# VectorE's block sums, folds and joins in a woven order, and product 5 of the last two batches in blocks

## The chip, the cores and the metric

The kernel runs on one core of one Trainium2 chip. The metric is the device time of one launch in microseconds (us), the median of repeated runs. The four engines that compute are TensorE (PE in the profile), VectorE (DVE), ScalarE (ACT) and GpSimd (POOL). Data moves in DMAs that are issued from the queues of SyncE (SP), of ScalarE and of GpSimd. Each engine works through its own list of instructions in the order in which the program emits them.

## The reference, cut to what matters

It is one cross attention over 8 batches. All arrays are float32: `x1` and `x2` are (8, 512, 1024), the inner width is D = 64.

```python
q = einsum('bcn,dc->bnd', x1, Wq) + bq
k = einsum('bcn,dc->bdn', x2, Wk) + bk[:, None]
v = einsum('bcn,dc->bdn', x2, Wv) + bv[:, None]
attn = softmax(einsum('bnd,bdm->bnm', q, k), axis=2)
return einsum('bcm,bnm->bcn', v, attn) + x1
```

## The kernel before, in words

**Two products per batch.** The kernel doesn't build v. For each batch it multiplies `x2` with the exponentials of the scores (stage "y", contraction 1024) and then `Wv` with the result (stage "o", contraction 512); the division by the softmax's sums falls in between, and the bias and `x1` are added at the end. Both stages cut their matrices into 2 x 2 quarters and use Winograd's form of Strassen's product: seven products of quarters in place of eight, named 1, 2, 6, 7, 5, 3, 4 in `MULT` (L355). The left operands are the quarters `11`, `12`, `21`, `22` of `x2` and their sums `S1` to `S4`; the right operands are the quarters of the exponentials `e` and their sums `T1` to `T4`. VectorE makes most of these sums.

**Blocks.** A stage-y product can be done plainly (`multiply`, L365: 16 matmul records of 128x512) or in blocks, which is the same seven-product form once more inside it: 28 records of 128x256. Blocks need eight more sums: four 128x256 ones on the left (`inner_left`, L412, each reading one or two made just before it) and three on the right (`inner_right`, L421: a 128x1024 one for `T1` and `T3` together, then `T2` from `T1`, then `T4` from `T2`). Their partial results go through two PSUM tiles, "chain" and "third", that share two buffers with the score tiles. `multiply_seeded` (L459) serves products 1, 2, 7, 3 and starts a pair of banks; `multiply_onto` (L489) serves 4 and 5 and adds to banks that are in use. Both return `complete`, one more VectorE sum. Before the change, product 5 runs in blocks in batches 1 to 5 only (`five` in `period`, L764), and plainly in batches 0, 6 and 7.

**The softmax.** Scores are taken for two halves `h` of the queries in four tiles each; ScalarE copies them to SBUF. VectorE folds the four tiles into a maximum with three steps of 128x1024 (`fold`, L242) and one of 128x512 (`fold_halves`, L250); GpSimd then takes the maximum over partitions (`highest`, L254). `lower` (L290) subtracts it, ScalarE exponentiates. Sums go the same way: for half 0, GpSimd's accumulating DMAs add the tiles (`add_tile`, L619) and VectorE folds once; for half 1 VectorE does the folds. `total` (L260) sums over partitions on GpSimd and sends the row to `few`, 4 numbers per partition. `invert` (L269) takes reciprocals of `few` on VectorE and sends them to DRAM; `spread` (L275) broadcasts them to all partitions; `shares` does both.

**The period.** `period` (L764) is emitted once per batch `s` and also holds the scores and exponentials of the next batch `n`, and the projections of queries and keys of the one after (`nn`). There are no due times and no planner: the order is written out by hand. TensorE's order in a middle batch is: products 1, 2, 6 of stage y; scores of half 0 of `n`; queries of `nn`; products 5, 7, 3; scores of half 1 of `n`; keys of `nn`; product 4; then the seven of stage o, in the order 1, 6, 2, 5, 7, 3, 4 (in the last batch 1, 6, 2, 5, 7, 4, 3). Batch 6 has no `nn`, so neither projection runs in it; batch 7 has no `n` either.

**Between the stages**, VectorE joins the seven results (`evict_y`, `evict_t3`, the two sums at the end of `multiply_4`), scales each quarter `y` by the reciprocals (`scale_y`, L544) and sums them (`sum_y`, L343). Product 2 of stage o reads the quarter `y["21"]`, which is joined last of all and scaled by `scale_y(s, "21")`.

Of the kernel before, what the change touches and what calls it, by code (L numbers as in the profile page):

```python
# [1 line left out]

# [9 lines left out]
ALU = mybir.AluOpType  # L12
# [3 lines left out]
def kernel(  # L16
# [47 lines left out]
    nc = tc.nc  # L64
# [81 lines left out]
    def sum_a(s, *ks):  # L146
        for k in ks:
            if k != "S3":
                s.a[k] = sb.tile([P, MH, C // 2], F32, tag=f"a{k}", name=f"a{k}_{s.b}")
        left_sums(s.a, *ks)  # L150
# [91 lines left out]
    def fold(s, h, i, kind, op):  # L242

        e = s.e[h]
        if i == 1:
            s.mx[h] = sb.tile([P, 2, H], F32, tag="fold", name=f"{kind}_{s.b}_{h}", bufs=2)
        f = s.mx[h]
        nc.vector.tensor_tensor(f, e[:, :, 0, :] if i == 1 else f, e[:, :, i, :], op)  # L248

    def fold_halves(s, h, op):  # L250
        f = s.mx[h]
        nc.vector.tensor_tensor(f[:, 0, :], f[:, 0, :], f[:, 1, :], op)  # L252

    def highest(s, h, halves=True):  # L254
        if halves:
            fold_halves(s, h, ALU.max)
        s.top[h] = sb.tile([P, H], F32, tag="top", name=f"top_{s.b}_{h}", bufs=2)
        nc.gpsimd.partition_all_reduce(s.top[h], s.mx[h][:, 0, :], P, ReduceOp.max)  # L258

    def total(s, h):  # L260
        fold_halves(s, h, ALU.add)
        s.den[h] = sb.tile([P, H], F32, tag="den", name=f"den_{s.b}_{h}", bufs=2)
        nc.gpsimd.partition_all_reduce(s.den[h], s.mx[h][:, 0, :], P, ReduceOp.add)  # L263
        s.few[h] = sb.tile([P, H // P], F32, tag="few", name=f"few_{s.b}_{h}", bufs=2)
        nc.gpsimd.dma_start(
            s.few[h], s.den[h][0:1, :].rearrange("o (p f) -> o p f", p=P)
        )
# [66 lines left out]
            s.tmp[1] = sb.tile([P, 2, H], F32, tag="yT1", name=f"uy1_{s.b}")  # L334
        nc.scalar.copy(s.tmp[1][:, j, :], s.bank["a", j])

    def sum_e(s, *ks, of=(0, 2)):
        for i in of:
            part = {n: v[:, i : i + 2, :] for n, v in s.t.items()}
            for k in ks:  # L340
                right_sums(part, k)

    def sum_y(s, k):  # L343
# [68 lines left out]
    def inner_left(s, i, x, tag):  # L412

        v = {f"{p + 1}{q + 1}": x[:, ts(q, MH // 2), ts(p, P)] for p in range(2) for q in range(2)}
        sums = sb.tile([P, 4, MH // 2, P], F32, tag=tag, name=f"aI{i}_{s.b}")
        for z, (k, x, y, op) in enumerate(LEFT):
            v[k] = sums[:, z]
            nc.vector.tensor_tensor(v[k], v[x], v[y], op)  # L418
        s.inner[i] = v

    def inner_right(s, i, x, *tags):  # L421

        v = {
            f"{q + 1}{r + 1}": x[:, ts(q, MH // 2), ts(r, H // 2)] for q in range(2) for r in range(2)
        }
        last = 4 // len(tags)
        shape = [P, last, MH // 2, H // 2]
        sums = [sb.tile(shape, F32, tag=t, name=f"eI{i}{t}_{s.b}") for t in tags]
        both, t2, t4 = sums[0][:, 0:2], sums[-1][:, last - 2], sums[-1][:, last - 1]
        part = x.rearrange("p (q k) (r n) -> p q k r n", q=2, r=2)  # L430
        nc.vector.tensor_tensor(
            both, part[:, :, :, 1, :], part[:, 0].rearrange("p k r n -> p r k n"), ALU.subtract
        )
        nc.vector.tensor_tensor(t2, both[:, 0], v["22"], ALU.subtract)
        nc.vector.tensor_tensor(t4, v["21"], t2, ALU.add)
        s.inner[i, "t"] = v | {"T1": both[:, 0], "T3": both[:, 1], "T2": t2, "T4": t4}

    def inner_product(s, i, z, ps, opens, *copies):

# [80 lines left out]
    def multiply_4(s, hooks={}):  # L520

        d, complete = multiply_onto(s, 4, "u5" if s.b < B - 1 else "a21", "r", hooks)
        complete()
        nc.vector.tensor_tensor(s.tmp[6], s.tmp[6], d, ALU.add)

    def multiply_5(s, hooks):

        d, complete = multiply_onto(s, 5, "u5", "r", hooks)
        complete()
        for j in range(2):  # L530
            nc.vector.tensor_tensor(d[:, j, :], s.bank["a", j], d[:, j, :], ALU.add)
        s.tmp[5] = d

    def copy_7(s, j):
        if j == 0:
# [8 lines left out]
    def scale_y(s, *ks):  # L544
        for k in ks:
            rden = s.rden[k in ("T3", "22")].unsqueeze(1).to_broadcast([P, 2, H])
            nc.vector.tensor_tensor(s.y[k], s.y[k], rden, ALU.mult)  # L547
# [77 lines left out]
        nc.scalar.copy(s.mx[h], s.e[h][:, :, 0, :])  # L625

    def sums(s, h):
        for i in range(1, MH):
            fold(s, h, i, "sum", ALU.add)
        total(s, h)  # L630

    def head_queries(s, x_sb, h, bank=None):
# [33 lines left out]
    def head(s):  # L666
# [55 lines left out]
        for i, bank in ((2, "a"), (3, "c")):  # L722
# [1 line left out]
            for g in range(2):  # L724
                nc.vector.tensor_tensor(f[:, 0, :], f[:, 0, :], copy.ps[g], ALU.max)
            copy()
        highest(s, 0, halves=False)
        sum_a(s, "S1", "S2")
        more_queries(*tiles[1:])
        load_x(states[1], x1)  # L730
# [11 lines left out]
    def head_second(s, n):  # L742


        scores(s, 1, 3)()
        for i in range(2, MH):
            fold(s, 1, i, "max", ALU.max)
        queries(n)()
        load_x(n, x2)
        highest(s, 1)  # L750
        sum_a(s, "S3", "S4")
        for i in range(MH):
            exponentials(s, 1, i)
# [10 lines left out]
    def period(s, n, nn, nnn):  # L764

        late = s.b >= 1
        five = late and nn is not None

        def first(i):
            multiply(s, "y", i, s.a, s.t, MH)  # L770
# [7 lines left out]
        def next_queries():  # L778
            evict = queries(nn, "c0")
            load_x(nn, x2)  # L780
            if five:
                return evict
            evict()

# [2 lines left out]
            if nnn:  # L787
                load_x(nnn, x1)

        def scores_0():  # L790
            then = scores_and(n, 0, 1, "c", next_queries if nn else nothing)
            for i in range(1, MH):
                fold(n, 0, i, "max", ALU.max)
            highest(n, 0)
            return then

# [11 lines left out]
        if s.b == 0:  # L808
            first(1)
            head_second(s, n)  # L810
            sum_e(s, "T1", "T2")
            total(s, 0)
            load_a(n, "11")
            first(2)
# [7 lines left out]
            load_a(n, "21", "22")  # L822
            first(6)
            scores_0()
            inner_left(s, 4, s.a["22"], "a12")
            inner_right(s, 4, s.t["T4"], "eT2")
            inner_left(s, 3, s.a["S4"], "aI3")
            shares(s, 1)
            first(5)
            inner_right(s, 3, s.t["22"], "eT1")  # L830
            for i in range(MH):
                lower(n, 0, i)
            first(7)
# [3 lines left out]
            complete_3()  # L837
            evict_t3(s)
            evict_y(s, "22")
            scale_y(s, "11", "T3", "22")  # L840
        else:
            complete_1 = multiply_seeded(s, 1, "y11")
            sum_e(s, "T1", "T2")
            complete_1()
            for i in range(1, MH):
                fold(s, 1, i, "sum", ALU.add)
            total(s, 1)
            invert(s, 0)
            complete_2 = multiply_seeded(
# [8 lines left out]
                sum_e(s, "T3")  # L858
            sum_t4(s)
            first(6)  # L860
            inner_left(s, 7, s.a["S3"], "yT4")
            if five:
                inner_left(s, 5, s.a["S1"], "i2")
                inner_right(s, 5, s.t["T1"], "y21", "u1")
            sum_a(s, "S4")
            if n:
                evict_q = scores_0()
            spread(s, 0)
            shares(s, 1)
            inner_right(s, 7, s.t["T3"], "yT1", "yT2")  # L870
            inner_left(s, 3, s.a["S4"], "aI3")
            if five:
                multiply_5(s, {6: evict_q})
            else:
                first(5)
            inner_right(s, 3, s.t["22"], "eT1")
            if n:
                lower(n, 0, 0)
            complete_7 = multiply_seeded(s, 7, "y12")
# [2 lines left out]
            if n:  # L882
                for i in range(1, MH):
                    lower(n, 0, i)
            else:
                inner_left(s, 4, s.a["22"], "a12")
                inner_right(s, 4, s.t["T4"], "eT2")

            hooks = {2: lambda: copy_7(s, 0), 5: lambda: copy_7(s, 1)}
            if n:  # L890
# [14 lines left out]
            if nn:  # L905
                next_keys()
        if late and n:
            inner_left(s, 4, s.a["22"], "a12")
            inner_right(s, 4, s.t["T4"], "eT2")
        if late:  # L910
            scale_y(s, "11", "T3", "22")
        sum_y(s, "T2")
        sum_y(s, "T1")
        if s.b == 0:
            value_sums("S1", "S2")
            for i in range(1, MH):
                fold(n, 1, i, "max", ALU.max)
            highest(n, 1)
        hooks = {}
        if s.b == 0:  # L920
# [1 line left out]
        elif n:  # L922
            hooks = {6: lambda: add_exponential(2), 5: lambda: exponential(n, 0, 3)}
            if nn is None:
                hooks[7] = first_sum
        multiply_4(s, hooks)
        if late and n:
            negate(n, "S3")
        if n:
# [1 line left out]
        if nn:  # L931
            load_a(nn, "21", "22")
        evict_y(s, "21")
        scale_y(s, "21")
        sum_y(s, "T4")
        if late and n:
            for i in range(1, MH):
                fold(n, 1, i, "max", ALU.max)
            highest(n, 1)
            add_11(n, "S3")  # L940
        second(1)
        if s.b == 0:
            copy_first(n, 0)
# [14 lines left out]
        evict_o(s, "11")  # L958
        if n:
            add_tile(n, 0, 3)  # L960
            inner_left(n, 1, n.a["11"], "i2")
        second(5)
        if n:
            for i in range(2 if s.b == 0 else 0, MH):
# [4 lines left out]
            add_11(n, "S2")  # L969
        evict_o(s, "22")  # L970
        if n:
            inner_right(n, 1, n.e[0][:, 0], "yT1", "yT2")
            inner_left(n, 2, n.a["12"], "aS4")
            inner_right(n, 2, n.e[0][:, 1], "eT4")
            second(3)
            evict_o(s, "12")
            second(4)
            total(n, 0)
            evict_o(s, "21")
        else:  # L980
            second(4)
            evict_o(s, "21")
            second(3)
            evict_o(s, "12")
# [37 lines left out]
```

## Time and profile before

| | us |
|---|---|
| median of 3 runs | 682.16 (682.11 to 682.16) |
| the profiled execution's own time | 682.56 |
| its span, first to last instruction | 680.8 |
| TensorE busy | 672.1 (99%) |
| VectorE busy | 615.2 (90%) |
| ScalarE busy | 336.9 (49%) |
| GpSimd busy | 218.5 (32%) |

The profiled execution is 0.40 us above the median, and 1.76 us of its time lie outside its span. TensorE's granted clock is 1.000 throughout. TensorE is busy in nine tenths or more of nearly every slice of the span, and so is VectorE in most; which of the two sets the time in a batch has to be read from the waits of that batch. In the timeline, a bracket behind an instruction holds the idle time of its engine before it and what ended that idle time. The numbering of batches is from 0.

### The profile page before, as it was taken

What the parts mean: (1) busy time and instruction counts of PE and PEld (TensorE: products, weight loads), DVE (VectorE), ACT (ScalarE), POOL (GpSimd) and SP (SyncE); (2) the same over time, 40 slices, a digit from 0 to 9 for tenths busy, and PEclk for the clock granted to TensorE, in tenths of its full rate; (3) what the DMA queues carried; (4) which work ended last, traced back from release to release, by engine and by line L of the source; (5) the groups of instructions that cost most, each with busy time, mean ns of one, the idle gap of its engine ahead of it and who ended that gap; (6) DMA issues with size and microseconds to landing.
All of it is one profiled execution on the core that took longest, in us unless ns stands there. A gap on an engine that the chain in (4) does not pass through costs nothing.

```text
span 680.8 us, 7209 instructions
## 1 busy us (share of the span) xinstructions
PE 672.1 (99%) x2420; PEld 397.9 (58%) x2420; DVE 615.2 (90%) x763; ACT 336.9 (49%) x564; POOL 218.5 (32%) x182
## 2 busy tenths in 40 slices
PE   8999999999999999999999999999999999999997
PEld 5333554757547565566656576464854747556763
DVE  1999998899999999999999998999989979999884
ACT  2734266365554564544644637446475356553320
POOL 0124215251153502643125421344213451154100
PEclk9999999999999999999999999999999999999999
DMA  9656658967798759969499693996947985489503
GB/s 300 271 191 241 155 212 139 240 138 246 180 249 221 154 202 253 214 185 245 123 297 199 174 264 116 280 212 160 277 89 174 222 194 110 92 146 268 144 13 110
DMA packets 50772, 131.09 MB, mean 193 GB/s; under 512 B 5552, under 2 KB 7856, under 8 KB 50736
## 3 DMA queue, kind: packets, MB, share of 16 engines
q0 software_dynamic: 22464, 54.60, 44.7%
q1 hardware_dynamic: 27984, 75.64, 30.8%
q10 hardware_dynamic: 288, 0.39, 0.2%
q8 instruction: 19, 0.31, 0.2%
q14 instruction: 17, 0.14, 0.1%
HBM read 87.30 MB, written 16.81 MB: 153 GB/s over the span
## 4 chain that ended last, share of the span: by engine, by line
PE 84%; DVE 6%; DMA 5%; issue 2%; ACT 1%; SPq 1%; POOL 1%; DVEq 0%; POOLq 0%; ACTq 0%
PE ps_ya L380 11%; PE ps_oa L380 11%; PE ps_yc L442 8%; PE ps_oc L380 7%; PE ps_ya L442 6%; PE ps_s L228 5%; PE ps_o L400 4%; PE ps_o L380 4%; PE ps_k L181 3%; PE ps_q L181 3%; PE ps_i4chain L442 3%; PE ps_i3chain L442 3%; PE ps_i7chain L442 2%; PE ps_i1chain L442 2%; PE ps_i2chain L442 2%
## 5 line engine op out<-in xcount | busy, mean ns | idle before, releaser
L263 POOL PARTITION_ALL_REDUCE den<-sum x16 | 52.6, 3285 | 97.4 <-DVE few L271 60.3
L258 POOL PARTITION_ALL_REDUCE top<-max x16 | 37.6, 2352 | 126.3 <-DVE max L252 75.7
L380 PE MATMUL ps_ya<-eT,aS 128*128 128x512 f32 x176 | 77.5, 594 | 0.0
L293 DVE TENSOR_TENSOR e<-e,top 128x1024 f32<-128x1024 f32 x60 | 69.9, 1218 | 0.0
L620 POOL DMA_DIRECT2D sum<-e x21 | 32.1, 1530 | 108.7 <-ACT sum L625 42.0
L297 ACT ACTIVATE e<-e 128x1024 f32<-128x1024 f32 x60 | 61.8, 1058 | 4.7 <-DVE e L293 4.0
L380 PE MATMUL ps_oa<-yT,w_S 128*128 128x512 f32 x128 | 57.5, 592 | 0.0
L380 PE MATMUL ps_oc<-yT,w 128*128 128x512 f32 x128 | 57.4, 592 | 0.0
L380 PEld LDWEIGHTS ps_ya<-eT,aS 128*128 128x128 f32 x176 | 33.2, 190 | 40.1 <-issue 37.9
L237 ACT COPY e<-ps_s 128x1024 f32<-128x1024 f32 x46 | 45.6, 1032 | 9.0 <-PE ps_s L228 8.8
L228 PE MATMUL ps_s<-q,k 64*128 64x512 f32 x188 | 47.9, 608 | 0.9 <-ACT q L647 0.8
L380 PEld LDWEIGHTS ps_oa<-yT,w_S 128*128 128x128 f32 x128 | 24.3, 190 | 30.6 <-issue 30.6
L380 PEld LDWEIGHTS ps_oc<-yT,w 128*128 128x128 f32 x128 | 24.3, 190 | 30.6 <-issue 29.2
L248 DVE TENSOR_TENSOR max<-max,e 128x1024 f32<-128x1024 f32 x30 | 36.7, 1225 | 2.2
L391 ACT COPY uo<-ps_oa 128x512 f32<-128x512 f32 x32 | 18.7, 586 | 34.9 <-PE ps_oa L380 34.9
L391 ACT COPY uy<-ps_ya 128x512 f32<-128x512 f32 x24 | 13.9, 588 | 36.8 <-PE ps_ya L380 36.8
L228 PEld LDWEIGHTS ps_s<-q,k 64*128 64x128 f32 x188 | 17.1, 186 | 24.5 <-issue 18.0
L479 ACT COPY ps_ya<-ps_i1chain 128x256 f32<-128x256 f32 x28 | 10.0, 357 | 42.2 <-PE ps_i1chain L442 38.7
L547 DVE TENSOR_TENSOR y<-y,den 128x1024 f32<-128x1024 f32 x24 | 29.3, 1221 | 0.3
L418 DVE TENSOR_TENSOR aI<-a 128x256 f32<-128x256 f32 x58 | 29.4, 547 | 0.0
L380 PE MATMUL ps_oa<-y,w_S 128*128 128x512 f32 (+1 forms) x68 | 28.8, 567 | 0.0
L400 PE MATMUL ps_o<-y,w 128*128 128x512 f32 x64 | 28.8, 592 | 0.0
(202 smaller groups left out, 1539.0 us busy)
## 6 DMA issues: line engine op xcount, KB each, us to landing
x_in_x_dram<-in_x_dram SPq DMA_DIRECT2D x60, 512.0 KB, 7.6
a<-in_x2T_dram SPq DMA_DIRECT2D x32, 512.0 KB, 10.1
sum<-e POOLq DMA_DIRECT2D x21, 512.0 KB, 10.1
aS<-in_x2T_dram POOLq DMA_DIRECT2D x14, 512.0 KB, 8.9
uo<-in_x_dram POOLq DMA_DIRECT2D x14, 512.0 KB, 9.9
r<-in_x_dram POOLq DMA_DIRECT2D x14, 512.0 KB, 12.2
out_dram<-r SPq DMA_DIRECT2D x14, 512.0 KB, 6.5
eT<-eT POOLq DMA_DIRECT2D x14, 512.0 KB, 10.1
```

Of the source, the lines that this page charges most:

```text
L181: nc.tensor.matmul(ps[r, :], w_sb[:, c, :], s.x[:, c, ts(h, H)], start=(c == 0), stop=(c == CT - 1),)
L228: nc.tensor.matmul(ps[g], s.k[r, ts(i, P)], s.q[r, ts(h, H)], start=True, stop=True)
L237: nc.scalar.copy(e[:, :, i, :], whole)
L248: nc.vector.tensor_tensor(f, e[:, :, 0, :] if i == 1 else f, e[:, :, i, :], op)
L258: nc.gpsimd.partition_all_reduce(s.top[h], s.mx[h][:, 0, :], P, ReduceOp.max)
L263: nc.gpsimd.partition_all_reduce(s.den[h], s.mx[h][:, 0, :], P, ReduceOp.add)
L293: nc.vector.tensor_tensor(e, e, top, ALU.subtract)
L297: nc.scalar.activation(e, e, AF.Exp)
L380: nc.tensor.matmul(ps[:, n], left[ka][:, k, ts(j, P)], right[kb][:, k, n], start=opens and k == 0, stop=i in (2, 3, 4) and k == n_k - 1, s ...
L391: nc.scalar.copy(s.tmp[i][:, j, :], ps)
L400: nc.tensor.matmul(ps, w["11"][:, k, ts(j, P)], s.y["11"][:, k, :], start=k == 0, stop=False, skip_group_check=True)
L442: nc.tensor.matmul(ps, s.inner[i][ka][:, k, :], s.inner[i, "t"][kb][:, k, :], start=opens and k == 0, stop=z in (2, 3, 4) and k == MH // 2 ...
```

## The change

It touches the order of instructions on VectorE, and one product in two batches. Sums, folds and joins are returned as lists of steps, and `weave` emits several such lists in turn, one step from each.

- **Second-level sums.** `inner_left` and `inner_right` of the same product, or of neighbouring ones, alternate. `sum_e` does both halves of one sum before the next sum. `scale_y` takes `T3` before `11`.
- **Sums of half 1** (batches 1 to 7): the folds alternate with `inner_left` of product 7, which moves up ahead of `complete_2` and `evict_y(s, "11")`.
- **Maxima of half 1** (batches 1 to 6): three folds and the fold of halves stood behind `sum_y(s, "T4")`; now the first stands between `sum_y` of `T2` and `T1`, two alternate with the two sums that end product 4, and the fold of halves stands ahead of `scale_y(s, "21")`. `inner_left` of the next batch's product 1 and `inner_right` of its product 2 move up to stand around `sum_y(s, "T4")`.
- **Product 5 in blocks** in batches 6 and 7 too; in batch 7 its sums stand ahead of the folds of half 1.

`fold_halves` is taken out of `highest` and `total` and called, or woven, by itself. Product 5 in batch 0 stays plain. The core of the diff:

```diff
+    def folds(s, h, kind, op):
+        return [lambda i=i: fold(s, h, i, kind, op) for i in range(1, MH)] + [lambda: fold_halves(s, h, op)]
+
+    def weave(*rows):
+        for steps in zip_longest(*rows):
+            for step in steps:
+                if step:
+                    step()
...
-    def sum_e(s, *ks, of=(0, 2)):
-        for i in of:
-            part = {n: v[:, i : i + 2, :] for n, v in s.t.items()}
-            for k in ks:
+    def sum_e(s, *ks):
+        parts = [{n: v[:, i : i + 2, :] for n, v in s.t.items()} for i in (0, 2)]
+        for k in ks:
+            for part in parts:
                 right_sums(part, k)
...
-            for i in range(1, MH):
-                fold(s, 1, i, "sum", ALU.add)
+            if n:
+                weave(folds(s, 1, "sum", ALU.add), inner_left(s, 7, s.a["S3"], "yT4"))
+            else:
+                weave(inner_left(s, 5, s.a["S1"], "i2"), inner_right(s, 5, s.t["T1"], "y21", "u1"))
+                weave(folds(s, 1, "sum", ALU.add), inner_left(s, 7, s.a["S3"], "yT4"))
             total(s, 1)
             invert(s, 0)
...
             first(6)
-            inner_left(s, 7, s.a["S3"], "yT4")
-            if five:
-                inner_left(s, 5, s.a["S1"], "i2")
-                inner_right(s, 5, s.t["T1"], "y21", "u1")
-            sum_a(s, "S4")
+            if n:
+                weave(
+                    inner_left(s, 5, s.a["S1"], "i2"),
+                    inner_right(s, 5, s.t["T1"], "y21", "u1"),
+                    [lambda: sum_a(s, "S4")],
+                )
+            else:
+                sum_a(s, "S4")
...
             shares(s, 1)
-            inner_right(s, 7, s.t["T3"], "yT1", "yT2")
-            inner_left(s, 3, s.a["S4"], "aI3")
-            if five:
-                multiply_5(s, {6: evict_q})
-            else:
-                first(5)
-            inner_right(s, 3, s.t["22"], "eT1")
+            weave(inner_right(s, 7, s.t["T3"], "yT1", "yT2"), inner_left(s, 3, s.a["S4"], "aI3"))
+            join_5 = multiply_5(s, {6: evict_q} if nn else {})
+            weave(join_5, inner_right(s, 3, s.t["22"], "eT1"))
...
         if late and n:
-            inner_left(s, 4, s.a["22"], "a12")
-            inner_right(s, 4, s.t["T4"], "eT2")
+            weave(inner_left(s, 4, s.a["22"], "a12"), inner_right(s, 4, s.t["T4"], "eT2"))
         if late:
-            scale_y(s, "11", "T3", "22")
+            scale_y(s, "T3", "11", "22")
         sum_y(s, "T2")
+        tops = folds(n, 1, "max", ALU.max) if n else []
...
+        if late and n:
+            tops.pop(0)()
         sum_y(s, "T1")
...
-        multiply_4(s, hooks)
+        join_4 = multiply_4(s, hooks)
+        weave(join_4, tops[:2] if late else [])
...
         evict_y(s, "21")
+        lefts_1 = rights_2 = []
+        if late and n:
+            tops[2]()
+            lefts_1 = inner_left(n, 1, n.a["11"], "i2")
+            rights_2 = inner_right(n, 2, n.e[0][:, 1], "eT4")
         scale_y(s, "21")
+        for step in lefts_1[:1]:
+            step()
         sum_y(s, "T4")
         if late and n:
-            for i in range(1, MH):
-                fold(n, 1, i, "max", ALU.max)
             highest(n, 1)
             add_11(n, "S3")
+            weave(rights_2, lefts_1[1:])
...
         if n:
-            inner_right(n, 1, n.e[0][:, 0], "yT1", "yT2")
-            inner_left(n, 2, n.a["12"], "aS4")
-            inner_right(n, 2, n.e[0][:, 1], "eT4")
+            rows = [inner_right(n, 1, n.e[0][:, 0], "yT1", "yT2"), inner_left(n, 2, n.a["12"], "aS4")]
+            if s.b == 0:
+                rows += [inner_right(n, 2, n.e[0][:, 1], "eT4")]
+            weave(*rows)
```

## The prediction

> **What bounds the kernel now.** I read the busy times first, then the PE timeline with its gaps (in brackets), the chain of waits for the batches' starts, and the DVE timeline of the batches with a gap.
>
> ```profile
> PE 672.1 (99%) x2420; PEld 397.9 (58%) x2420; DVE 615.2 (90%) x763; ACT 336.9 (49%) x564; POOL 218.5 (32%) x182
> ...
> 167.94 1.29 PE L228 MATMUL ps_sa<-q,k 64*128 64x512 f32 x3 [0.89 <-DVE yT L542]
> ...
> 579.29 1.13 PE L442 MATMUL ps_i4third<-eI4eT,aI 128*128 128x256 f32 x4 [0.29 <-ACT e L237]
> ```
>
> PE is the bound: behind 50 us its timeline has these two gaps and no other. In batches 2 to 5 it runs without one (by the chain, product 6 starts at 298.50, 380.49 and 462.67, 82.0 to 82.2 us apart). So a shorter DVE list is worth only the two places where PE waits. Batch 1: scores at 165.05 to keys at 170.44 take 5.39 us, in batch 2 248.80 to 252.48, 3.68 us: 1.71 us lost, behind `evict_t3`. Batch 6: scores to the start of stage o take 10.56 (574.24 to 584.80), in batch 2 without the keys 3.68 + 6.14 = 9.82: 0.7 lost to ACT's copies.
>
> The DVE timeline shows what weaving is worth:
>
> ```profile
> 501.79 1.22 DVE L547 TENSOR_TENSOR yT<-yT,den 128x1024 f32<-128x1024 f32 x1
> 502.92 1.22 DVE L547 TENSOR_TENSOR y<-y,den 128x1024 f32<-128x1024 f32 x1
> 504.06 1.22 DVE L348 TENSOR_TENSOR yT<-y,yT 128x1024 f32<-128x1024 f32 x1
> 505.31 1.23 DVE L350 TENSOR_TENSOR yT<-y,yT 128x1024 f32<-128x1024 f32 x1
> ...
> 507.53 0.69 DVE L516 TENSOR_TENSOR d<-d,v 128x512 f32<-128x512 f32 x1 [0.99 <-ACT d L451]
> ```
>
> Starts are 1.13 to 1.14 apart where an instruction doesn't read the one before, 1.25 where it does (504.06 to 505.31): 0.11 us for each dependent pair. By the same reading a 128x512 takes 0.61 or 0.72, a 128x256 0.34 or 0.45. The last line shows DVE waiting for PE's product 4 anyway: in a middle batch it has slack.
>
> **Batch 1, a gain.** The chain of waits runs on DVE from 124.56 (the last accumulated sum lands) to 167.9. Savings up to `complete_3`: `sum_e` 0.12; the stretch from 132.84 to 146.40 (13.56) becomes folds with `inner_left` 7 (3 x 1.14 + 0.61 + 4 x 0.34 = 5.39), reciprocal 0.09, `complete_2` 0.58, `evict_y` 1.19, and left 5, right 5 and `S4` woven (4 x 0.34 + 2 x 1.14 + 2 x 0.61 = 4.86), 12.11: 1.45 saved; right 7 with left 3 4.64 for 4.87, joins with right 3 4.23 for 4.38. Together 1.95, against 1.71 wanted: the gap closes, **-1.71**. In the batches behind it PE has no gap to close: 0, if nothing new comes late.
>
> **What comes late: `y["21"]`.** Output product 2 needs it scaled. The change puts three folds (1.14 each) and a fold of halves (0.61), 4.03, ahead of it; woven, the same stretch loses about 0.9 of dependent pairs. Middle batch: `complete_4` stays at 507.53, since ACT releases it; then 0.61 + 1.14 (fold) + 1.22 (join) + 1.14 (fold) + 1.2 (`evict_y`) + 0.61 = 513.45, scaled by 514.67. Product 2 starts at 515.24 in the PE timeline: 0.57 spare, where it was 3.1. Cost 0, but the cover is thin.
>
> Batch 6 has no projections, so DVE there has 7 us less to hide in, and now makes seven sums for product 5 as well:
>
> ```profile
> 554.80 1.23 DVE L248 TENSOR_TENSOR max<-e 128x1024 f32<-128x1024 f32 x1 [3.27 <-ACT e L235]
> ...
> 573.88 0.70 DVE L485 TENSOR_TENSOR ps_ya<-ps_ya,v 128x512 f32<-128x512 f32 x1 [0.59 <-ACT ps_ya L479]
> ...
> 585.65 0.68 DVE L516 TENSOR_TENSOR d<-d,v 128x512 f32<-128x512 f32 x1
> ...
> 589.02 1.22 DVE L547 TENSOR_TENSOR y<-y,den 128x1024 f32<-128x1024 f32 x1
> ...
> 591.67 3.60 PE L380 MATMUL ps_o<-y,w 128*128 128x512 f32 x8
> ```
>
> The last two lines are the scaling of `y["21"]` and the product that reads it: 1.43 us spare today (590.24 to 591.67). The seven sums (3.72) hide in the 3.27 of idle and in the weave: I get DVE free at 554.06, so 554.80 stays. From there it is contiguous: folds and reciprocal 4.61; right 7 and left 3 4.64, of which 0.7 is a hold beside GpSimd's reduction, as at 560.64 today; `complete_5` 0.60; joins with right 3 3.63; `lower` 1.14; `complete_7` and `evict_y` 1.79; three `lower` 3.41; `complete_3` 0.60; `evict_t3` 1.20; left 4 with right 4 3.72; three scalings 3.40; `T2`, fold, `T1` 3.42; `complete_4` 0.61; fold, join, fold 3.51; `evict_y` 1.19; halves 0.61; scaling 1.22: 39.3, so 594.1. Product 2 starts **2.45** later than today, whatever PE has won before.
>
> **Product 5 in blocks.** Plain it takes 7.0 us (555.09 to 562.06), in blocks 28 records at 0.2157, 6.04 (product 7: 562.06 to 568.11): 0.84 to 0.97 less. In batch 6 it must first wait some 0.5 for the copies of the scores, like the 579.29 line above, so 0.3 is left; the wait for `y["21"]` swallows it. ACT gets five 0.36 copies for two of 0.59, behind PE.
>
> **Batch 7.**
>
> ```profile
> 624.09 0.69 DVE L252 TENSOR_TENSOR sum<-sum 128x512 f32<-128x512 f32 x1
> ...
> 628.41 0.59 POOL L265 DMA_DIRECT2D few<-den  x1 [0.30 <-POOL den L263]
> ...
> 633.30 0.18 DVE L271 RECIPROCAL few<-few 128x4 f32<-128x4 f32 x1 [1.24 <-DMA few<-den]
> 633.40 1.20 DVE L431 TENSOR_TENSOR eI7yT<-e 128x1024 f32<-128x1024 f32 x1
> ...
> 659.65 3.60 PE L380 MATMUL ps_o<-y,w 128*128 128x512 f32 x8
> ```
>
> `few` comes 8.52 us behind the end of the fold of halves (624.78), and DVE already waits 1.24 for it, with right 7 queued behind. The change puts the seven sums of product 5 (3.72) and left 7 (1.0) ahead of that fold. The start is anchored by a landing and not by PE: the last `sum<-e` today lands at 612.0; its three neighbours on GpSimd's queue can start 2 us earlier in batch 6 (the maximum is folded sooner), so I take 610.3. Behind GpSimd's reduction of it, DVE's first sum runs at about 613.2 (614.9 today). Then 14.1 to the end of the fold, 627.3; `few` at 635.85; right 7 at 635.95. From there DVE is contiguous to the scaled `y["21"]`: right 7 with left 3 3.83, `complete_5`, joins, right 3 4.24, `complete_7` and `evict_y` 1.8, left 4 with right 4 3.72, `complete_3`, `evict_t3` 1.8, scalings 3.4, `T2`, `T1` 2.4, `complete_4` and join 2.0, `evict_y` 1.3, scaling 1.22: 25.8, so 661.7. PE, late by 2.45 and 0.84 shorter, comes there at 661.3. So the loss carried to the end is 661.7 - 659.65 = **2.1**: batches 6 and 7 overlap and don't add. If `few` lands faster it is 1.6 (PE alone); with the old landing, 614.9, it is 3.2.
>
> The accumulations for `T4` stand behind `total` and `invert` on GpSimd's queue and go out 4 us later in batch 7; right 4 is far behind them.
>
> **The sum.** -1.71 + 2.1 = +0.4, on the profiled 682.56 and, less its 0.40, on the median: 682.6. With the ends above, and 0.4 either way on the 39.3: 681.7 to 684.1.
>
> **The rivals.**
>
> A. *PE stays the bound everywhere.* Speaks for it: in every middle batch DVE idles before `complete_3`, and the change removes DVE time. Against: no idle is left in my 39.3. If 2.5 us are missing from that list's true length: -1.71 - 0.3 - 0.84 = -2.85, 679.3.
>
> B. *Batch 7 waits for `few` in full* (slower). If the accumulated sum moves with PE instead of landing sooner, it lands at 612.0 + 2.4; then all DVE work above, counted from 614.9 + 2.4, puts the scaled `y["21"]` at 665.9, 6.2 late: +4.5, 686.7. It decides from the point where the sum lands behind 611. For it: that queue has four transfers of 512 KB within 2.6 us, and one of them waits for output product 2. Against: it is emptied in order, and the first two don't wait for PE.
>
> C. *The thin cover in batches 1 to 5 fails.* GpSimd's reduction of the maximum now starts beside the scaling of `y["21"]`. Today the second DVE instruction behind that fold is held:
>
> ```profile
> 517.08 0.69 DVE L252 TENSOR_TENSOR max<-max 128x512 f32<-128x512 f32 x1
> 517.69 1.59 DVE L418 TENSOR_TENSOR aI<-a 128x256 f32<-128x256 f32 x2
> ...
> 517.87 1.89 POOL L258 PARTITION_ALL_REDUCE top<-max  x1 [9.05 <-DVE max L252]
> ```
>
> The pair takes 1.59 instead of 0.76; the first, issued before GpSimd started, isn't held. So the scaling should pass. If it is the one held, by 0.8 to 1.0, five batches lose 0.45 each and batch 6 1.0: about 685.3. The Trainium skill (SBUF — State Buffer, section "SBUF: two separate sides") says that whichever of the two starts first has the shared ports for its whole instruction; the trace agrees as to who goes first, though DVE went on 0.9 us before the reduction's span ended.
>
> D. *Weaving saves nothing per instruction.* No row speaks for it; two rows above give 0.11. Then batch 1 keeps its gap, the 39.3 grows by some 1.3, and batch 7 by 2: 686. The Trainium skill (VectorE: DVE Perf Modes, section "The DRAIN you can't avoid") says that the next operation waits for the pipe to empty whether or not a semaphore stands between them; by that rule this rival would hold. The 1.14 beside 1.25 in this trace contradicts it.
>
> **Chances.** The forecast 0.45, A 0.20, B 0.17, C 0.10, D 0.05, other slower stalls 0.03. Less than 0.2% (1.36 us) can hardly be told from no change: A is faster; the forecast is within that but for its uppermost edge (0.03); the rest is slower: 0.20, 0.42, 0.38. The range reaches from A's 679.2 past C to 686.0, leaving out the full price of B.
>
> **What would show it.** Right: no gap before `ps_sa` in batch 1; dependent pairs gone from the folds; a PE gap before output product 2 of batch 6 of over 2 us, ended by DVE L547; in batch 7 a longer DVE wait for `few`, and at most a short PE gap at product 7 or output product 2. Wrong: output product 2 on time in batch 6, or gaps before it in batches 1 to 5; product 7 of batch 7 over 1.5 us late; batch 1 still with its gap.

## The result, and the profile after

The changed kernel takes **683.64 us** (median of 8 runs, 683.22 to 684.41), the kernel before on the same chip 682.07: ratio 1.0027, 95% interval 1.0016 to 1.0038, or 1.57 us slower. The profiled execution took 684.41 us with a span of 682.6. (Of the experiments below, one run of `e5_only5`, 784 us, and one of `e7_best`, 785 us, had a granted clock of 0.85 and are left out of the medians; the first was the profiled one, so `e5_only5` ran again as `e5b_only5`.)

The busy times of the changed kernel, and under them all gaps of its TensorE timeline behind 50 us:

```profile
PE 672.3 (98%) x2444; PEld 402.4 (59%) x2444; DVE 602.6 (88%) x783; ACT 337.7 (49%) x570; POOL 224.5 (33%) x182
...
553.97 1.13 PE L456 MATMUL ps_i5chain<-eT,aS 128*128 128x256 f32 x4 [0.50 <-ACT e L238]
592.30 3.70 PE L389 MATMUL ps_o<-y,w 128*128 128x512 f32 x8 [1.81 <-DVE y L563]
...
636.81 1.10 PE L456 MATMUL ps_i7third<-eI7yT,aI 128*128 128x256 f32 x4 [1.22 <-DVE eI7yT L445]
```

VectorE has 20 more instructions and is busy 12.6 us less (615.2 before): the weave takes dependent pairs away. (The weave alone, with as many instructions as before, is busy 598.7.) The gap of batch 1 is gone and three new ones stand in batches 6 and 7. The time between fixed points of the TensorE timeline says what each is worth. The points are the starts of stage-y product 6 and of output products 1 and 2, in us; the rows below the second are the experiments. Each time is compared with the kernel before on the same chip, which took 681.95 to 682.25 there.

| kernel | product 6 of batch 1 to that of 2 | batch 6: product 6 to output 1 | output 1 to output 2 | output 2 to product 6 of batch 7 | batch 7: product 6 to output 2 | time, ratio to before [95% interval] |
|---|---|---|---|---|---|---|
| before | 83.74 | 40.30 | 6.87 | 29.25 | 38.73 | 682.07 |
| after | 81.99 | 40.66 | 8.84 | 29.36 | 39.70 | 683.64, 1.0027 [1.0016, 1.0038] |
| e1_maxima_back | 81.99 | 40.65 | 6.87 | 29.25 | 39.28 | 681.38, 0.9993 [0.9984, 1.0002] |
| e2_plain5 | 81.99 | 40.30 | 8.45 | 29.35 | 38.73 | 682.00, 0.9998 [0.9989, 1.0007] |
| e3_gaps | 82.00 | 40.65 | 8.84 | 29.36 | 37.91 | 682.26, 1.0003 [0.9994, 1.0012] |
| e4_weave_only | 81.99 | 40.30 | 6.87 | 29.25 | 38.73 | 680.57, 0.9976 [0.9967, 0.9985] |
| e5b_only5 | 83.68 | 41.61 | 6.87 | 29.25 | 46.72 | 691.19, 1.0139 [1.0125, 1.0153] |
| e6_one_gap | 82.00 | 40.66 | 8.84 | 29.36 | 37.91 | 682.27, 1.0002 [0.9993, 1.0011] |
| e7_best | 81.99 | 40.30 | 6.87 | 29.25 | 40.12 | 681.40, 0.9993 [0.9984, 1.0002] |
| e8_not_held | 81.99 | 40.31 | 6.86 | 29.26 | 38.65 | 679.90, 0.9972 [0.9961, 0.9982] |
| e9_two_folds | 81.99 | 40.30 | 6.87 | 29.25 | 37.99 | 679.74, 0.9967 [0.9954, 0.9979] |
| e4b_weave_only | 82.00 | 40.30 | 6.87 | 29.25 | 38.73 | 680.29, 0.9973 [0.9963, 0.9984] |

Before against after: 1.75 won in batch 1; in batch 6 0.36 and 1.97 lost, then 0.11, in batch 7 0.97. That is 3.41 lost for 1.75 won. The profiles reach the first of these points anywhere from 131.5 to 132.9 us, and two executions of one kernel (e4 and e4b) differ by 0.7 there, which is why stretches are compared and not absolute positions.

**Batch 6 in the changed kernel.** VectorE, then GpSimd, then VectorE again:

```profile
553.10 1.22 DVE L249 TENSOR_TENSOR max<-e 128x1024 f32<-128x1024 f32 x1 [3.71 <-ACT e L236]
...
590.43 0.68 DVE L253 TENSOR_TENSOR max<-max 128x512 f32<-128x512 f32 x1
591.03 1.22 DVE L563 TENSOR_TENSOR y<-y,den 128x1024 f32<-128x1024 f32 x1
...
591.22 7.50 POOL L268 PARTITION_ALL_REDUCE top<-max  x1 [3.54 <-DVE max L253]
598.59 0.92 POOL L172 DMA_DIRECT2D a<-in_x2T_dram  x1
...
598.75 4.63 DVE L302 TENSOR_TENSOR e<-e,top 128x1024 f32<-128x1024 f32 x4 [1.68 <-POOL top L268]
...
612.85 0.69 DVE L253 TENSOR_TENSOR sum<-sum 128x512 f32<-128x512 f32 x1 [4.35 <-DMA sum<-e]
```

From 553.10 to the end of the scaling, 592.25, VectorE has no idle time: 39.15 us, and output product 2 starts when it ends. Then comes what was not foreseen. GpSimd's reduction of the maximum takes 7.50 us; in batches 1 to 5 this reduction of half 1 takes 2.29 to 2.68. It ends only after VectorE has run out of work and waits for it (1.68). Behind it on GpSimd's queue stand four transfers, the last of them an accumulation of the sum of half 0; the first goes out 7.4 us behind the start of the reduction. So the accumulated sum lands late: VectorE idles 4.35 for it (1.10 before) and folds it at 612.85.

**Batch 7.** GpSimd sends `few`, VectorE inverts it and makes right 7; the last line is the kind of transfer, with its size and the time from issue to landing between 620 and 640 us:

```profile
633.39 0.59 POOL L274 DMA_DIRECT2D few<-den  x1 [0.30 <-POOL den L272]
...
635.38 0.18 DVE L280 RECIPROCAL few<-few 128x4 f32<-128x4 f32 x1
635.48 1.19 DVE L445 TENSOR_TENSOR eI7yT<-e 128x1024 f32<-128x1024 f32 x1
...
660.08 1.23 DVE L563 TENSOR_TENSOR y<-y,den 128x1024 f32<-128x1024 f32 x1
...
few<-den POOLq DMA_DIRECT2D x1, 2.0 KB, 2.0
```

The reciprocal has no bracket: VectorE reached it only at 635.38 and `few` was there. It landed 2.0 us after its issue; in the kernel before, this transfer took 4.9, with 338 GB/s of other traffic around it (626 to 632 us) where the changed kernel had 141 (632 to 638). Right 7 is late, TensorE waits 1.22 for it, and from there VectorE's list leads up to output product 2 at 661.36.

### The profile page after: what moved, and what is told of

It reads as the page before. It is cut to its first block, busy times and chain, and to the rows that moved or that the text cites. A ratio compares the mean times of both kernels' runs of the same rounds, so it can differ in the third digit from the quotient of the medians.

```text
span 682.6 us, 7284 instructions
## 1 busy us (share of the span) xinstructions
PE 672.3 (98%) x2444; PEld 402.4 (59%) x2444; DVE 602.6 (88%) x783; ACT 337.7 (49%) x570; POOL 224.5 (33%) x182
## 4 chain that ended last, share of the span: by engine, by line
PE 85%; DVE 7%; DMA 3%; issue 3%; ACT 1%; POOL 1%; SPq 0%; DVEq 0%; POOLq 0%; ACTq 0%
PE ps_oa L389 10%; PE ps_ya L389 9%; PE ps_ya L456 7%; PE ps_yc L456 7%; PE ps_oc L389 7%; PE ps_s L229 6%; PE ps_q L182 4%; PE ps_o L389 4%; PE ps_k L182 3%; PE ps_o L409 3%; PE ps_i4chain L456 3%; PE ps_i3chain L456 3%; PE ps_i5chain L456 2%; PE ps_i7chain L456 2%; PE ps_i1chain L456 2%
## 5 line engine op out<-in xcount | busy, mean ns | idle before, releaser
L268 POOL PARTITION_ALL_REDUCE top<-max x16 | 44.5, 2779 | 103.4 <-DVE max L253 51.4
L636 POOL DMA_DIRECT2D sum<-e x21 | 28.5, 1356 | 117.0 <-ACT sum L641 45.8
L389 PE MATMUL ps_ya<-eT,aS 128*128 128x512 f32 x144 | 63.5, 594 | 0.0
L389 PEld LDWEIGHTS ps_ya<-eT,aS 128*128 128x128 f32 x144 | 27.2, 190 | 32.1 <-issue 29.5
L389 PE MATMUL ps_o<-y,w 128*128 128x512 f32 x64 | 29.0, 595 | 1.9 <-DVE y L563 1.8
L249 DVE TENSOR_TENSOR max<-e 128x1024 f32<-128x1024 f32 x15 | 18.3, 1220 | 12.4 <-ACT e L236 12.3
L409 PE MATMUL ps_o<-y,w 128*128 128x512 f32 x64 | 28.8, 592 | 0.0
```

Source lines behind the costliest of these rows:

```text
L389: nc.tensor.matmul(ps[:, n], left[ka][:, k, ts(j, P)], right[kb][:, k, n], start=opens and k == 0, stop=i in (2, 3, 4) and k == n_k - 1, s ...
L409: nc.tensor.matmul(ps, w["11"][:, k, ts(j, P)], s.y["11"][:, k, :], start=k == 0, stop=False, skip_group_check=True)
```

## The experiments

**e1_maxima_back.** The maxima of half 1, left 1 and right 2 go back to their old places.

```diff
-        if late and n:
-            tops.pop(0)()
...
-        weave(join_4, tops[:2] if late else [])
+        weave(join_4)
...
-        lefts_1 = rights_2 = []
-        ...
         scale_y(s, "21")
-        for step in lefts_1[:1]:
-            step()
         sum_y(s, "T4")
         if late and n:
+            weave(tops)
             highest(n, 1)
             add_11(n, "S3")
-            weave(rights_2, lefts_1[1:])
```

> Everything of the change except the move of the half-1 maxima: three folds and the fold of halves stand behind the sum T4 again, left 1 and right 2 at their old places. Theory (the folds ahead of y 21 make output product 2 of batch 6 late, and batch 7 starts from a sum that lands late): the 1.8 us gap of batch 6 is gone (2.0 us), GpSimd's maximum reduction of batch 6 takes under 3 us instead of 7.5, the sum lands 2 us sooner, and of batch 7's loss about half is left: 681.4 us (680.9 to 682.0). Rival P (the extra sums of product 5 alone make both batches late): the gap in batch 6 stays above 1.3 us, 683 us or more. Rival S (only the long reduction costs): the gap in batch 6 stays, 0.9 us comes back in batch 7, 682.7 us.

681.38, as expected. No gap before output product 2 of batch 6 (6.87), and GpSimd's reduction takes 1.88 us there. In batch 7 TensorE still waits 0.80 for right 7 and the stretch is 39.28: there the blocks of product 5 cost VectorE more than they save TensorE.

**e2_plain5.** Product 5 plain again in batches 6 and 7; the maxima stay where the change put them.

```diff
-            join_5 = multiply_5(s, {6: evict_q} if nn else {})
+            if nn:
+                join_5 = multiply_5(s, {6: evict_q})
+            else:
+                first(5)
+                join_5 = []
```

(and without the sums of product 5 in these batches)

> Everything of the change except product 5 of batches 6 and 7, which is plain again. Theory: VectorE loses the 1.8 us of joins in batch 6 and 5.5 us in batch 7, TensorE gains 0.3 and 0.84 us of work; y 21 of batch 6 comes at about 590.5 us, just before output product 2, so the gap there is under 0.3 us, and batch 7 has none: 681.0 us (680.6 to 681.6). Rival P (product 5 alone is the cause) gives the same here and differs in the first kernel. Rival S (only the long reduction): the gap of batch 6 stays at 1.5 us or more, 682.5 us.

682.00, 1.0 above the expectation. The gap in batch 6 nearly stays:

```profile
510.85 7.50 POOL L268 PARTITION_ALL_REDUCE top<-max  x1 [5.13 <-DVE max L253]
...
590.58 3.70 PE L389 MATMUL ps_o<-y,w 128*128 128x512 f32 x8 [1.41 <-DVE y L563]
```

The expectation had counted the 1.8 us of removed joins and the completion as if they brought the scaling forward. They don't: behind them `complete_3` waits for ScalarE's copy (0.67 of idle), so the list is counted from 571.21, and from there to the end of the scaling it takes 19.3 us with the maxima ahead, 16.4 in the kernel before. The maxima alone make the gap; beside the changed kernel's 1.81, the blocks add 0.4 to it. The first line shows the long reduction in batch 5 too, where it costs nothing; it stands in batch 6 as well, and without the blocks batch 7 loses nothing (38.73).

**e3_gaps.** Right 2 and the rest of left 1 behind `sum_y(s, "T4")` one after the other instead of woven; nothing else.

```diff
-            weave(rights_2, lefts_1[1:])
+            for step in rights_2 + lefts_1[1:]:
+                step()
```

> The change, with one edit: right 2 and the rest of left 1, behind the fold of the maximum, are emitted one list after the other, so that four of those six instructions read their neighbour's result again and VectorE has gaps. Theory (VectorE's unbroken stream keeps GpSimd's reduction from its SBUF ports for 5 us in batch 6): the reduction takes under 5 us there instead of 7.5, the sum lands 1 to 2 us sooner, batch 7's gap of 1.2 us shrinks below 0.5: 682.4 to 683.2 us; the gap of 1.8 us in batch 6 stays. Rival (the reduction is long for another reason): 7.5 us stays and the time is 683.6 us.

682.26, 1.4 us below the changed kernel with more VectorE time (605.8 us busy for 602.6). The reduction falls less than expected (5.29, not under 5) and the time a little more (682.4 was the lower end). The reduction in batch 6, and the first VectorE instruction behind its start that reads its neighbour's result:

```profile
590.98 5.29 POOL L268 PARTITION_ALL_REDUCE top<-max  x1 [3.50 <-DVE max L253]
...
594.65 1.41 DVE L448 TENSOR_TENSOR eI2eT<-eI2eT,e 128x512 f32<-128x512 f32 x1
```

At that instruction the reduction gets in: the instruction takes 1.41 where this shape takes 0.68. The accumulated sum is folded at 610.18, TensorE has no gap in batch 7, and the blocks of product 5 bring their 0.82 (37.91).

**e4_weave_only.** e1 and e2 together: the weave, no maxima moved, no blocks added. It ran again as **e4b_weave_only** beside a later kernel.

> The weave without the move of the maxima and with product 5 plain in batches 6 and 7. Theory: only batch 1's gap is closed, 1.7 us, and nothing comes late: 680.4 us (680.0 to 680.9), no TensorE gap of VectorE's making. Rival D (weaving saves nothing on VectorE): 682.1 us with the gap in batch 1 as before.

> The kernel of e4_weave_only unchanged, on the same chip as e9_two_folds, so that the blocks of batch 7 can be read as a difference: both theories 680.4 to 680.6; e9_two_folds should be 0.7 to 1.2 below it by the theory, and not below it by the rival.

680.57, as expected, and 680.29, 0.1 below its range. Only batch 1 differs from the kernel before, by 1.75 us, and that is the time won. It refutes the rival that weaving saves nothing. Beside e2 it prices the move of the maxima: 1.4 us of time, and 1.58 in the stretch from output 1 to output 2 (8.45 for 6.87).

**e6_one_gap.** Two neighbours of the changed kernel change places.

```diff
         scale_y(s, "21")
+        sum_y(s, "T4")
         for step in lefts_1[:1]:
             step()
-        sum_y(s, "T4")
```

> The changed kernel with two neighbours on VectorE swapped: sum_y of T4 directly behind the scaling of y["21"] that it reads, and the first of left 1's sums behind it; nothing removed. Theory (GpSimd's reduction of the maximum in batch 6 is kept from starting by VectorE's unbroken run, and the first dependent pair lets it in): the reduction's record takes 3.5 us or less in place of 7.50, the accumulated sum is folded by 610.5 in place of 612.85, no TensorE gap at product 7 of batch 7, and the time is that of the kernel with right 2 and left 1 unwoven or a little less, 681.9 to 682.4; the gap before output product 2 of batch 6 stays at 1.8. Rival (one dependent pair is too short to let it in, or it was the length of the unwoven stretch that counted): 5 us or more, 683.0 to 683.7.

682.27, as expected. The same work in the same stretch, one dependent pair more:

```profile
590.47 2.68 POOL L268 PARTITION_ALL_REDUCE top<-max  x1 [3.46 <-DVE max L253]
...
591.53 1.94 DVE L359 TENSOR_TENSOR yT<-y,yT 128x1024 f32<-128x1024 f32 x1
...
607.86 0.69 DVE L253 TENSOR_TENSOR sum<-sum 128x512 f32<-128x512 f32 x1 [1.04 <-DMA sum<-e]
```

The reduction falls from 7.50 to 2.68 (it takes 2.21 to 2.68 in batches 1 to 6), and it is now `T4` that is held (1.94 for 1.22). Everything on GpSimd's queue follows, the sum is folded at 607.86, and batch 7 keeps the blocks' gain. The gap in batch 6 stays at 1.81: it is not the reduction's doing. The profile is of one execution, but the times say that the hold and its end are steady: all 8 runs of the changed kernel took 683.22 or more, all 11 of this one 682.75 or less, on chips where the kernel before took 682.07 and 682.00.

**e5_only5 and e5b_only5.** The kernel before with product 5 in blocks in the last two batches, nothing woven.

```diff
-        five = late and nn is not None
+        five = late
...
-                multiply_5(s, {6: evict_q})
+                multiply_5(s, {6: evict_q} if nn else {})
```

> The kernel before, with product 5 in blocks in batches 6 and 7 and nothing else. Theory (the blocks are paid by VectorE where its list is unbroken): in batch 6 the seven sums take 4.2 us unwoven against 3.27 us of idle, then one more completion and two joins, 1.8: the scaled y["21"] comes 2.1 later (0.59 of idle is used up) against 1.43 spare, output product 2 is 0.7 late. In batch 7 it is 6.0 more between the accumulated sum and the scaled y["21"], against 1.24 + 0.2 of idle and 1.0 spare: 3.6 late, less nothing. Sum: 682.1 + 3.6 to 4.3, so 685.7 to 686.4, a bound by VectorE in both batches. Rival (the blocks by themselves save TensorE 0.84 in each batch, as the prediction's rival A has it): 680.4. Rival (only batch 7 pays, by `few` alone): 683.5.

> The kernel of e5_only5 unchanged: its three comparable runs gave 691.5, 5 us above the expectation, and its profile was taken at a granted clock of 0.85, where VectorE's waits cannot be read. Theory of before: 685.7 to 686.4, the three runs having been disturbed. Rival: 691.5 is real, and the profile shows TensorE gaps of some 9 us; if it is a held or starved reduction as in the changed kernel, they stand in batches 6 and 7 behind `top` or `few`; if it is the score copies, at product 5 of batch 6.

691.45 and, run again, 691.19: real, and 5 us above the expectation. In batch 6 the loss is 1.31, at product 5 and the scores of half 1, not at output product 2. In batch 7, VectorE's list, TensorE's records, and the windows with the granted clock (PEclk, last but two):

```profile
633.48 1.22 DVE L431 TENSOR_TENSOR eI5y<-eT 128x1024 f32<-128x1024 f32 x1
...
628.15 1.03 PE L442 MATMUL ps_i5chain<-eT,aS 128*128 128x256 f32 x4
634.75 2.07 PE L442 MATMUL ps_i5third<-eI5y,aI 128*128 128x256 f32 x4 [5.58 <-DVE eI5y L431]
...
634.70:638.00 3.30, 3.25 (x8) 2.62 (x9) 3.23 (x5) 0.37 (x1) 0.87 (x2) 0.50 0.95 195
638.00:641.00 3.00, 3.00 (x9) 2.41 (x8) 2.90 (x6) 0.37 (x1) 0.77 (x2) 0.53 0.22 73
641.00:645.00 4.00, 4.00 (x21) 3.51 (x20) 2.98 (x6) 1.07 (x4) 0.00 (x0) 1.00 0.22 66
```

Product 5's sums stand behind the folds of half 1, `T3` and left 7. The expectation had counted only the list's total; the first right-hand sum is wanted at 629 and made at 634.7. TensorE waits 5.58 us and then runs at half its clock for some 6, which costs some 3.1 more (four groups of four records take 6.53 from 634.75 to 641.28, where groups start 0.86 apart elsewhere). So the blocks in batch 7 need an earlier place for these sums, and the changed kernel gives them one, ahead of the folds.

**e7_best.** The weave alone, plus product 5 in blocks in batch 7 only, its sums behind the folds of half 1; one fold moved into the idle time of batch 6. Beside what is shown, right 7 goes ahead of the second reciprocal of `few` in batch 7, and `S4` and left 3 behind it.

```diff
+            if nn is None:
+                fold(n, 1, 1, "sum", ALU.add)
             fold_halves(n, 0, ALU.add)
             total(n, 0)
...
+                weave(folds(s, 1, "sum", ALU.add)[1:], inner_left(s, 7, s.a["S3"], "yT4"))
...
             if n is None:
+                weave(inner_left(s, 5, s.a["S1"], "i2"), inner_right(s, 5, s.t["T1"], "y21", "u1"))
                 sum_e(s, "T3")
```

> The weave alone (maxima of half 1 at their old place, product 5 plain in batch 6), plus product 5 in blocks in batch 7 alone, with its sums behind the folds of half 1 instead of ahead of them, the first of these folds moved into VectorE's idle time before the accumulated sum lands in batch 6, and right 7 ahead of the reciprocal of `few`. Theory (in batch 7 VectorE's list from the accumulated sum to the scaled y["21"] decides, and the blocks pay only where its idle time takes their sums): 5.5 us more work against 1.5 + 2.9 + 1.3 of idle in the kernel with the weave alone and 0.9 spare, so TensorE's 0.84 are kept: 679.6 to 680.0. Rival (VectorE has no such room): a gap before output product 2 of batch 7 and 680.6 or more.

681.40, 1.4 above the expected range, the rival's side: 40.12 in batch 7.

```profile
621.73 2.80 DVE L429 TENSOR_TENSOR aI<-a,aI 128x256 f32<-128x256 f32 x2
...
621.91 3.33 POOL L272 PARTITION_ALL_REDUCE den<-sum  x1 [6.84 <-DVE sum L253]
...
659.62 3.70 PE L389 MATMUL ps_o<-y,w 128*128 128x512 f32 x8 [0.79 <-DVE y L563]
```

Two sums of 128x256 that take 0.8 together took 2.80. They stand right behind the fold that starts GpSimd's reduction and are held until it is nearly over: they end 0.7 us ahead of its record. In e4_weave_only the instructions behind the start of that reduction are a reciprocal and sums that read an operand from PSUM, and they are not held.

**e8_not_held.** The last two of these sums go ahead of the fold of halves.

```diff
-                weave(folds(s, 1, "sum", ALU.add)[1:], inner_left(s, 7, s.a["S3"], "yT4"))
+                fold_2, fold_3, halves = folds(s, 1, "sum", ALU.add)[1:]
+                weave([fold_2, fold_3], inner_left(s, 7, s.a["S3"], "yT4"))
+                halves()
```

> The kernel of e7_best with one change of order in batch 7: the fold of halves of half 1 comes behind all four sums of left 7 instead of ahead of the last two; the reciprocal of the first `few` and the two joins that read PSUM now stand next to it. Theory (in e7_best the pair of 128x256 sums at 621.73 took 2.80 us in place of 0.8, held by GpSimd's reduction that started at 621.91, and this hold is the whole of the missing gain): the sums are not held, the scaled y["21"] of batch 7 comes 1.5 to 2.1 us earlier, no TensorE gap ahead of it but at most 0.2 at product 5, and the time is 679.7 to 680.2. Rival (the hold only moves to the sums of product 5 behind the joins, or VectorE's list is too long anyway): 680.8 or more.

679.90, in the expected range. The hold is gone but for 0.4 and batch 7 is 1.47 shorter (38.65). The expectation of no gap ahead of output product 2 missed:

```profile
623.51 0.84 DVE L429 TENSOR_TENSOR aI<-aS 128x256 f32<-128x256 f32 x1
...
657.25 3.70 PE L389 MATMUL ps_o<-y,w 128*128 128x512 f32 x8 [0.58 <-DVE y L563]
```

So by the profile the blocks gain only 0.1 here over the weave alone.

**e9_two_folds.** The second fold goes to batch 6 as well.

```diff
-                fold_2, fold_3, halves = folds(s, 1, "sum", ALU.add)[1:]
-                weave([fold_2, fold_3], inner_left(s, 7, s.a["S3"], "yT4"))
+                fold_3, halves = folds(s, 1, "sum", ALU.add)[2:]
+                weave(inner_left(s, 7, s.a["S3"], "yT4"), [nothing, fold_3])
                 halves()
...
                 fold(n, 1, 1, "sum", ALU.add)
+                fold(n, 1, 2, "sum", ALU.add)
             fold_halves(n, 0, ALU.add)
```

> The kernel of e8_not_held with the second fold of half 1's sums moved as well, from batch 7 to ahead of the fold of halves in batch 6, where VectorE still idled 0.7 us for the accumulated sum. e8_not_held has a TensorE gap of 0.58 left ahead of output product 2 of batch 7, and by its profile gains only 0.1 in batch 7 over the weave alone (38.65 us from product 6 to output product 2, for 38.73). Theory (VectorE's list from the accumulated sum to the scaled y["21"] decides): 1.14 us less in that list, 0.4 of it given back where the accumulated sum is folded later, so 0.7 earlier: the gap of 0.58 is gone, the stretch is 38.0 to 38.1, the time 679.2 to 679.6. Rival (the later fold of the accumulated sum delays its reduction and T2 of product 6 as much): no gain or a new gap at product 6, 679.9 to 680.6.

679.74 (679.43 to 680.37). No gap is left in batch 7 and its stretch is 37.99, 0.74 below the weave alone, as expected. The time is 0.1 above the expected range, and 0.55 below e4b_weave_only beside it where 0.7 to 1.2 was expected. The two runs' intervals overlap: a gain of less than 0.2% is not shown by the times, only by the stretch. This version and the weave alone both beat both kernels.

## Why the prediction was right or wrong

The range held the time, and batch 1 and batch 6 went by the mechanisms named. In batch 7 the prediction had the right bound, VectorE's list from the accumulated sum on, but missed what delayed its start. The likeliest case was placed within 0.2% and the time came 0.27% slower, just past that bound. Part of the closeness is luck: two errors in batch 7, of 4.25 and 2.80 us, point opposite ways. By its steps:

- **Batch 1, -1.71**: -1.75. Right, and e4_weave_only shows that the weave alone gives it. Rival D is refuted.
- **Batches 2 to 5, the thin cover of 0.57**: right, no gap, and 0.68 is left in batch 5 (512.87 to 513.55). Rival C fails as the prediction argued: the scaling, issued ahead of the reduction, passes, and the sum behind it is held. Batch 5, VectorE, GpSimd and TensorE:

```profile
511.65 1.22 DVE L563 TENSOR_TENSOR y<-y,den 128x1024 f32<-128x1024 f32 x1
512.78 1.26 DVE L429 TENSOR_TENSOR aI<-a 128x256 f32<-128x256 f32 x1
...
511.83 2.68 POOL L268 PARTITION_ALL_REDUCE top<-max  x1 [4.88 <-DVE max L253]
...
513.55 3.60 PE L389 MATMUL ps_o<-y,w 128*128 128x512 f32 x8
```

- **Batch 6, output product 2 late by 2.45**: 0.36 + 1.97 = 2.33; the list of 39.3 us from 554.80 was 39.15 from 553.10. Right, and e1 and e2 show its cause: the maxima ahead of the scaling make 1.58 by themselves, the blocks on top of them the rest. Rival A, TensorE bound everywhere, needed a list 2.5 us shorter.
- **Product 5 in batch 6, 0.3 left**: wrong in sign. The wait of 0.50 for the score copies was as foreseen, and product 7 starts 0.20 sooner than without blocks. But `evict_t3` comes later behind VectorE's joins, and TensorE's scores of half 1 wait for it: product 6 to output 1 is 0.36 longer with blocks (e1, 40.65) than without (e2, 40.30). It is small.
- **Batch 7, a carried loss of 2.1**: 3.41. This is the term that was mis-sized, and the step that failed is the landing of the accumulated sum, taken at 610.3 because "its three neighbours on GpSimd's queue can start 2 us earlier". They started later, behind the reduction of 7.50 us, which the prediction had left at its length of before (1.88). In the coordinates of before (the changed kernel is 1.70 ahead at product 6 of batch 6) the sum was folded at 614.55, 4.25 later than forecast. That is rival B's condition, a sum behind 611, by another cause than B named. B's price of 6.2 us did not come, because `few` came 5.72 or less behind the fold instead of 8.52, 2.80 less; VectorE's wait for it, which was to grow, is gone. The two errors leave 4.25 - 2.80 = 1.45; measured is 1.3 (scaled `y["21"]` at 661.31, forecast 661.7 - 1.70 = 660.0).

  e6_one_gap removes the cause. Its sum is folded at 607.86, which is 610.31 in the coordinates of before (it is 2.45 ahead at product 6 of batch 6), as forecast; its carried loss is 0.36 + 1.97 + 0.11 - 0.82 = 1.62, the 1.6 that the prediction gives for a faster `few`; and its time is 0.27 above the kernel before in place of 1.57. So the move of the maxima does bring the sum forward, and in the changed kernel the long reduction takes that back.

  One sum of the prediction is off. With VectorE's first sum at 614.9 in place of 613.2, all that follows is 1.7 later, and its list gives a carried loss of 3.8, not 3.2; the upper end of 684.1 would be 0.6 higher.
- **The sum**, each kernel less the one before on its chip: the weave alone -1.5 (e4), the moved maxima +1.4 (e2 less e4), the blocks +1.7 (after less e2), of which 1.3 is the held-back reduction (after less e6). The forecast of +0.4 had the first right and the other two together at 2.1 for 3.1. The held-back reduction costs only together with the blocks: in e2_plain5 it stands in batch 6 at 7.50 too, and batch 7 loses nothing.

## What to carry to other kernels

Count an order change on one engine also for another engine that it can hold up: idle moments that look like waste can be what lets the other start (here one dependent pair, 7.50 us to 2.68). Weave where the list sets the time, but don't put new work ahead of the one result that the next engine waits for. An added block of sums must be placed by when its first result is wanted, not by the total of the list.

## What the hardware showed that was not expected

- A run of VectorE instructions with two SBUF operands and no dependent pair can hold up a GpSimd reduction until the run ends: 7.50 us for 2.68, and 5.29 where the first dependent pair came 3.7 us into it. One such pair placed 1.1 us behind the start let it in at once. The Trainium skill (SBUF — State Buffer, section "SBUF: two separate sides") says that whichever of the two starts first gets the shared ports for its whole instruction and the other blocks. The held pair of 2.80 us in e7_best agrees as to who goes first, though it ended 0.7 us ahead of the reduction's record; that the waiting reduction loses to each next VectorE instruction is seen only in these runs. What stays open: the same list let the reduction in at once in batches 1 to 5 of the changed kernel and not in batch 6, and in e2_plain5 not in batch 5 either. Counted from the scaling, the reduction starts within 0.02 us of the same point in both cases (batch 4 apart, where it starts 0.4 to 0.7 later), so it may be a matter of timing below what the trace resolves; this was not tried.
- After 5.58 us without work TensorE ran at a granted clock of 0.50 for some 6 us (e5b_only5), where gaps of up to 1.81 us left it at 1.00. The Trainium skill (TensorE: Matmul & The Clock Gate, section "HAM oscillation — how this bites in real kernels") says to leave no idle gap over about 3.4 us; these two gaps lie on either side of that and agree.
- The same 2 KB transfer of `few` took 4.9 us in one order and 2.0 in another: 2.0 in the four kernels in which product 5's sums stand ahead of the folds of half 1 in batch 7 (after, e1, e3, e6), 4.5 to 5.6 in the others. The other traffic beside it differs too (338 and 141 GB/s above); what makes the difference was not tried.
